# Two levels of Strassen's scheme for a GRU's input products, the inner sums continued in PSUM by ScalarE

## The chip, the cores and the metric

The kernel runs on one core of a Trainium2 chip. The metric is the device time of one execution in microseconds (us). Five engines work at once, each on its own queue of instructions: PE (TensorE, matrix products), DVE (VectorE), ACT (ScalarE), POOL (GpSimd) and SP, which here only starts DMAs. PE reads its operands from the on-chip memory SBUF and writes its products to PSUM; DVE and ACT can read and write both.

## The reference, cut to what matters

Two layers with residual connections. Layer 0 is a gated recurrence that can be computed as a scan over time. Layer 1 is a GRU over 128 steps for 64 batches with width 512, and the change lies there:

```python
xz = jnp.einsum('btd,de->bte', seq, W_z)     # likewise xr with W_r, xh with W
def step(h, xs):
    xzt, xrt, xht = xs
    z = jax.nn.sigmoid(xzt + h @ U_z + vz)   # vz, vr, vh: conditioning and biases
    r = jax.nn.sigmoid(xrt + h @ U_r + vr)
    hh = jnp.tanh(xht + r * h @ U + vh)
    h_new = (1.0 - z) * h + z * hh
    return (h_new, h_new)
```

The products of `seq` (the output of layer 0) with the three weights don't depend on the recurrence and can be made ahead of it. Everything is float32.

## The kernel before, in words

**Layer 0** runs over 16 groups of four batches and four chunks of 128 features (the loop at the file's end). PE multiplies (L186), ACT takes sigmoids, DVE the norm and scans, and the sum x + hidden goes to a DRAM tensor `x2d`, from where it comes back in windows of TW = 16 steps (`load_window`, L469).

**Layer 1** is cut into two streams of 32 batches. Their steps alternate, stream 1 two steps behind. In a step's tiles the partitions are four quarters q of the width by 32 batches, and the free dimension holds j blocks of 32 features. A product with a block of 128 rows of a weight is four matmuls, one for each q, into 32 partitions each (L376); on the chip each float32 matmul is two instructions. `gather` copies four steps of x out of a window into `x4` (ACT) and takes the sums of blocks that Strassen's scheme (in Winograd's form) needs (`s4`, four POOL instructions).

**One step** (`Stream.step`) issues to PE the products of h for r and z into the stream's accumulator `g`, then a fill, then the products of r*h for the candidate. Between them stand ACT's sigmoid (L594), DVE's product r*h (L596) and its transpose (L597), which the candidate's products need. After them come ACT's tanh (L623), `put_share` (L554, the ready share of x for the stream's next step, copied into `g`), DVE's new h and its transpose (L638). `pin` keeps every engine's instructions in the order of the code.

**The fill** makes products of x for later steps. `queue_pair` treats two steps at once as the rows of a 2x2 block matrix, the two halves of the width as its columns, and forms seven products instead of eight; a product is two units of four matmuls with 192 columns (three gates of 64). `fill` issues seven units a step. The products go to halves of PSUM tiles that `product_psum` deals out in turn: a new tile's first half, then its second. One step later DVE (L519) and POOL (L522) add them up to the shares `xz`; `to_read` holds these reads.

The weights' differences for the scheme (`winograd_weights`) are made by DVE in layer 0, one a chunk (L678). The first steps (stream 0 up to 3, stream 1 up to 1) don't use the scheme: `put_v` copies the conditioning into `g`, and `x_products` multiplies x directly, 32 instructions of 384 columns. Where there is nothing to fill with, `idle_products` multiplies zeros.

Ordering between engines is inserted by the framework from the tiles that each instruction reads and writes.

Of the kernel before, what the change touches and what calls it, by code (L numbers as in the profile page):

```python
# [18 lines left out]
def kernel(  # L19
# [23 lines left out]
):  # L43

# [208 lines left out]
    spare = []  # L253

    def chunk_norm(g, c, between=None):
# [17 lines left out]
        if spare:  # L273
            beside.append(spare.pop(0)())
# [51 lines left out]

    def conditioning():

        bias1 = const.tile([P, 3, P], F32, name="bias1")
# [23 lines left out]

        vs = []
        for s in range(2):
            whole = const.tile([P, 3, P], F32, name=f"whole_v{s}")
            pin(nc.vector.tensor_tensor(whole, ps[s], bias1, ALU.add))
            v = const.tile([P, 2, 3, HP], F32, name=f"v{s}")
            halves = whole.rearrange("p g (n e) -> p n g e", n=2)
            pin(nc.scalar.copy(v[:, 0], halves[:, 0]))  # L360
            pin(nc.vector.tensor_tensor(v[:, 1], halves[:, 1], halves[:, 0], ALU.subtract))
            vs.append((whole, v))
# [4 lines left out]
    TW = 16  # L367
# [3 lines left out]
    def matmuls(p, lhsT, w, start=True, stop=True):  # L371

        for k, wk in enumerate(w):
            for q in range(Q):
                pin(
                    nc.tensor.matmul(  # L376
                        p[q * SB : (q + 1) * SB],
                        lhsT=lhsT(k),
                        rhs=part(wk, q),
                        start=(start and k == 0),  # L380
                        stop=(stop and k == len(w) - 1),
                        skip_group_check=True,
                    )
                )

    def winograd_weights():
# [8 lines left out]
        differences = []  # L395
        for k in range(HC):
            differences += [
                (t1[k], b12[k], b11[k]),
                (t2[k], b22[k], t1[k]),
                (t3[k], b22[k], b12[k]),  # L400
                (t4[k], b21[k], t2[k]),
            ]
        return (b11, b21, b22, t1, t2, t3, t4), iter(differences)

    banks = []

    def product_psum():
        if banks:
            return banks.pop()
        n = product_psum.n = product_psum.n + 1  # L410
        p = psum.tile([P, 2, 3, HP], F32, tag=("p1", "p2", "tp")[n % 3], name=f"m{n}")
        banks.append(p[:, 1])
        return p[:, 0]

    product_psum.n = 0
    to_fill = []
    to_read = []

    def fill(n):
        n = min(n, len(to_fill))  # L420
        for _ in range(n):
            unit, reads = to_fill.pop(0)
            unit()
            to_read.extend(reads)
        return n

    def idle_products(n):

        if n:
            p = product_psum()  # L430
            for _ in range(n):
                matmuls(p, lambda _: zeros, w_products[0][:1])

    def read_all():
        while to_read:
            to_read.pop(0)()

    class Stream:
        def __init__(self, s):
# [10 lines left out]

            self.x4 = [const.tile([P, 4, P], F32, name=f"x4_{s}_{n}") for n in range(2)]
            self.s4 = [const.tile([P, 4, 2, HP], F32, name=f"s4_{s}_{n}") for n in range(2)]
            self.windows = {}

        def take_scratch(self, scratch):

            n = 6 * P
            self.xz = [
                scratch[:, m * n : (m + 1) * n].rearrange("p (t g e) -> p t g e", t=2, g=3)
                for m in range(2)  # L460
            ]
            self.sums = scratch[:, 2 * n : 3 * n].rearrange("p (n g e) -> p n g e", n=4, g=3)
# [13 lines left out]
        def gather(self, n):  # L476
            for instruction in self.gather_parts(n):
                instruction()

        def gather_parts(self, n):  # L480

# [3 lines left out]
            x4, s4 = self.x4[n % 2], self.s4[n % 2]  # L485
# [5 lines left out]
            blocks = x4.rearrange("p (m t) (i e) -> p t i m e", t=2, i=2)  # L491
            a11, a12, a21, a22 = (blocks[:, t_, i] for t_ in range(2) for i in range(2))
            s1, s2, s3, s4_ = (s4[:, m] for m in range(4))
            return [
                lambda a=a: pin(nc.gpsimd.tensor_tensor(*a))
# [5 lines left out]
                )  # L501
            ]

        def queue_pair(self, m):

            n, pair = m // 2, m % 2
            x4, s4 = self.x4[n % 2], self.s4[n % 2]
            c1, c2 = (
                [self.xz[m % 2][:, t, :, i * HP : (i + 1) * HP] for i in range(2)] for t in range(2)
            )  # L510
            u, s5, w, u3 = (self.sums[:, i] for i in range(4))
            v1, v21 = self.v[:, 0], self.v[:, 1]
            b11, b21, b22, t1, t2, t3, t4 = w_products

            def block(t, i):
                return x4[:, 2 * pair + t, i * HP : (i + 1) * HP]

            def add(dst, p, other):
                return lambda: pin(nc.vector.tensor_tensor(dst, p, other, ALU.add))  # L519

            def add_beside(dst, a, b_):
                return lambda: pin(nc.gpsimd.tensor_tensor(dst, a, b_, ALU.add))  # L522

            def product(a, w_, reads):
                p = []

                def unit(k):
                    if k == 0:
                        p.append(product_psum())
                    matmuls(  # L530
                        p[0], lambda _: a[:, k * SB : (k + 1) * SB], w_[k : k + 1],
                        start=(k == 0), stop=(k == HC - 1),
                    )

                for k in range(HC):
                    last = k == HC - 1
                    to_fill.append(
                        (
                            (lambda k=k: unit(k)),
                            [lambda: [f() for f in reads(p[0])]] if last else [],  # L540
                        )
                    )

            product(block(0, 0), b11, lambda p: [add(u, p, v1)])
            product(block(0, 1), b21, lambda p: [add(c1[0], p, u)])
            product(s4[:, 1, pair], t2, lambda p: [add(u, p, u)])
            product(s4[:, 0, pair], t1, lambda p: [add(s5, p, v21)])
            product(s4[:, 3, pair], b22, lambda p: [add(w, p, s5), add_beside(c1[1], w, u)])
            product(s4[:, 2, pair], t3, lambda p: [add(u3, p, u), add_beside(c2[1], u3, s5)])
            product(block(1, 1), t4, lambda p: [add(c2[0], p, u3)])  # L550

        def put_share(self, t):

            pin(nc.scalar.copy(self.g, self.xz[t // 2 % 2][:, t % 2]))  # L554
# [16 lines left out]
        def step(self, t, n_fill=7, idle=(0, 0), share=True, filler=None, between=None):  # L571
# [5 lines left out]
            reads = to_read[:]  # L577
            to_read.clear()

            def read(n):  # L580
                for _ in range(min(n, len(reads))):
                    reads.pop(0)()
# [4 lines left out]
            else:  # L587
# [7 lines left out]
                read(1)  # L595
# [4 lines left out]
                pin(nc.gpsimd.tensor_tensor(r, r, h_, ALU.mult))  # L600
            if filler:
                filler()
            fill(n_fill)
# [6 lines left out]
            read(len(reads) - 1)  # L610
# [13 lines left out]
            read(1)  # L624
            if share and t + 1 < S:
# [15 lines left out]
            self.store(t)  # L641

            if t % 4 == 0 and t + 8 <= S and (t > 0 or self.s == 1):
                self.gather(t // 4 + 1)
            if t % TW == 4 and t + TW < S:
                self.load_window(t // TW + 1)
# [17 lines left out]
    for g in range(NG):  # L664
        for c in range(K):
# [10 lines left out]
            if g >= 3:  # L676
                for dst, a, b_ in itertools.islice(sums_of_weights, 1):
                    pin(nc.vector.tensor_tensor(dst, a, b_, ALU.subtract))  # L678
# [5 lines left out]
        if g == 0:  # L684
# [3 lines left out]
            w_products, sums_of_weights = winograd_weights()  # L688
# [5 lines left out]
        if g == NG - 3:  # L694
            spare += streams[0].gather_parts(1)
# [6 lines left out]
    for st in streams:  # L702
        st.take_scratch(flat[:, st.s * 18 * P :])
# [7 lines left out]
    st0.step(0, n_fill=0, share=False)  # L711
# [7 lines left out]
    def step_1(rest):  # L719
        st0.g = g1  # L720
        st0.step(1, n_fill=0, share=False, filler=x_of_step_2, between=rest)
# [5 lines left out]
    st0.queue_pair(2)  # L727
    fill(7)
    st0.step(2, share=False, between=lambda: chunk_retained(g, c))
# [11 lines left out]
    st1.x_products(0)  # L741
    LEAD = 2
    for t in range(LEAD, S + LEAD):
        near_end = t >= S - 3
        n_fill = 4 if near_end else 7
        if t == LEAD + 1:

            st0.step(t, filler=lambda: st1.x_products(1))
        elif LEAD < t < S:
            st0.step(t, n_fill, idle=(0 if to_fill else 4, 0))  # L750
        elif t >= S:
            read_all()

# [43 lines left out]
```

## Time and profile before

| | us |
|---|---|
| median of 3 runs (lowest, highest) | 1974.89 (1974.46, 1975.33) |
| the profiled execution | 1976.27 |
| its span, first to last instruction | 1974.4 |
| first fill of the recurrence, tile m (start) | 722.7 |
| one step of one stream, tanh to tanh | 4.87 |

The page gives the span, each engine's busy time, and the span in 40 slices (a digit is the busy share in tenths; a slice is 49 us). Groups are named by line of the code, engine, operation and tiles; "128*32 128x192" for a matmul is a stationary operand of 128 rows by 32 columns and a moving one of 128 by 192. Timeline rows have the start, the time from the first start to the last end, the engine, the line, the operation, out<-in, the form, the count of merged instructions, and in brackets the engine's idle time before, with what ended it. Tile names are the program's without their numbers: `m` a product, `g` an accumulator, `W` the scratch that `xz` and `sums` live in, `f` the tiles of r, z and r*h.

### The profile page before, as it was taken

Reading aid. Unit: us, or ns where it says so; the run is one execution under the profiler, and the core shown is the slowest. Engines: PE = TensorE matmul, PEld = TensorE weight load, DVE = VectorE, ACT = ScalarE, POOL = GpSimd, SP = SyncE. Lnnn points to the kernel's source line nnn. Section 1 sums busy time; section 2 is a strip of 40 time slices with the busy share of each in tenths; the row PEclk is TensorE's granted clock in tenths of the full one; section 3 lists DMA queues with packets and bytes.
Section 4 is the critical chain, followed back from the end, with each engine's and each line's share of the span. In section 5 each row is a group of like instructions: output and inputs, shape, how many; then the busy total and the mean of one; then the engine's idle time right before and its main releaser. Section 6 shows DMA issues by size and latency. Waiting matters only on the chain.

```text
span 1974.4 us, 73723 instructions
## 1 busy us (share of the span) xinstructions
PE 1958.9 (99%) x32729; PEld 1412.5 (72%) x32729; DVE 1360.5 (69%) x2996; ACT 484.6 (25%) x1108; POOL 752.4 (38%) x1476
## 2 busy tenths in 40 slices
PE   9999999999999999999999999999999999999998
PEld 5444444444444447788888888888888888888887
DVE  6799999999999985555555555555555555555554
ACT  3222212122221222222222222222222222222222
POOL 1222222222233234444444444444444444444443
PEclk9999999999999999999999999999999999999999
DMA  6411111211111211201200220221120121110111
GB/s 202 157 48 48 48 43 54 64 59 49 48 48 43 77 37 24 59 15 19 60 16 14 41 41 14 37 39 20 35 41 14 19 57 19 17 17 14 19 19 19
DMA packets 228407, 84.64 MB, mean 43 GB/s; under 512 B 205484, under 2 KB 205496, under 8 KB 228088
## 3 DMA queue, kind: packets, MB, share of 16 engines
q1 hardware_dynamic: 227488, 79.85, 16.4%
q8 instruction: 257, 4.21, 0.9%
q14 instruction: 62, 0.51, 0.1%
q10 hardware_dynamic: 600, 0.07, 0.0%
HBM read 46.34 MB, written 33.55 MB: 40 GB/s over the span
## 4 chain that ended last, share of the span: by engine, by line
PE 70%; DVE 27%; issue 1%; DMA 1%; ACT 0%; DVEq 0%; SPq 0%; POOL 0%; ACTq 0%; POOLq 0%
PE g L376 34%; PE m L376 29%; DVE h L261 9%; PE p L186 6%; DVE h L312 3%; DVE i L295 3%; DVE h L302 3%; DVE i L294 2%; DVE i L307 2%; DVE f L279 2%; DVE i L282 2%; DVE h L260 2%; DMA cw<-in_L_cond_C_dram 1%; PE tp L144 1%; DMA x<-in_x_dram 0%
## 5 line engine op out<-in xcount | busy, mean ns | idle before, releaser
L186 PE MATMUL p<-xT,W 128*128 128x512 f32 (+1 forms) x1560 | 669.4, 586 | 0.7 <-issue 0.5
L186 PEld LDWEIGHTS p<-xT,W 128*128 128x128 f32 x1560 | 290.0, 190 | 341.7 <-issue 336.4
L376 PE MATMUL g<-w_s,h 128*32 128x256 f32 x8128 | 527.8, 379 | 1.1 <-DVE h L638 1.1
L376 PEld LDWEIGHTS g<-w_s,h 128*32 128x32 f32 x8128 | 336.4, 110 | 98.1 <-ACT g L554 1.8
L376 PE MATMUL m<-w_t,s 128*32 128x192 f32 x6000 | 376.7, 326 | 0.0
L376 PE MATMUL g<-w_s,f 128*32 128x128 f32 x8128 | 311.5, 273 | 2.5 <-DVE f L597 1.5
L630 DVE TENSOR_TENSOR h<-h,f 128x128 f32<-128x128 f32 x254 | 74.3, 292 | 343.7 <-ACT h L623 343.7
L640 POOL TENSOR_TENSOR o<-o,h 128x128 f32<-128x128 f32 x254 | 116.4, 458 | 475.2 <-DVE h L636 466.2
L376 PEld LDWEIGHTS m<-w_t,s 128*32 128x32 f32 x6000 | 263.6, 110 | 21.5 <-issue 0.4
L376 PEld LDWEIGHTS g<-w_s,f 128*32 128x32 f32 x8128 | 270.1, 110 | 10.8 <-issue 4.2
L623 ACT ACTIVATE h<-g 128x128 f32<-128x128 f32 x256 | 70.9, 277 | 697.7 <-PE g L376 697.7
L261 DVE RECIPROCAL h<-h 128x517 f32<-128x517 f32 x64 | 217.0, 3391 | 2.2
L519 DVE TENSOR_TENSOR W<-m,W 128x192 f32<-128x192 f32 x625 | 202.3, 339 | 20.3 <-PE m L376 3.2
L376 PE MATMUL m<-w_x,x 128*32 128x192 f32 x4000 | 206.8, 326 | 0.0
L265 POOL COPY first<-condT 128x4 f32<-128x4 f32 x64 | 12.1, 190 | 508.6 <-DVE h L260 494.0
L596 DVE TENSOR_TENSOR f<-f,h 128x128 f32<-128x128 f32 x254 | 86.2, 339 | 146.9 <-ACT f L594 146.9
L376 PEld LDWEIGHTS m<-w_x,x 128*32 128x32 f32 x4000 | 164.0, 110 | 21.2 <-issue 0.4
L281 ACT ACTIVATE f<-f 128x512 f32<-128x512 f32 x64 | 40.4, 631 | 452.6 <-DVE f L279 452.6
L599 POOL TENSOR_SCALAR f<-f 128x128 f32<-128x128 f32 x254 | 75.5, 297 | 195.6 <-DVE f L596 195.6
L594 ACT ACTIVATE f<-g 128x256 f32<-128x256 f32 x254 | 97.3, 383 | 201.1 <-PE g L376 198.2
L522 POOL TENSOR_TENSOR W<-W 128x192 f32<-128x192 f32 x250 | 143.5, 595 | 1.6 <-DVE W L519 1.5
L376 PE MATMUL m<-w_x,s 128*32 128x192 f32 x2000 | 125.8, 326 | 0.0
(79 smaller groups left out, 2008.2 us busy)
## 6 DMA issues: line engine op xcount, KB each, us to landing
x<-in_x_dram SPq DMA_DIRECT2D x64, 256.0 KB, 3.0
x2d<-x SPq DMA_DIRECT2D x63, 256.0 KB, 2.0
out_dram<-o SPq DMA_DIRECT2D x248, 64.0 KB, 2.0
xw<-x2d SPq DMA_DIRECT2D x60, 256.0 KB, 4.8
w_rows<-in_L_cond_W_f_dram SPq DMA_DIRECT2D x4, 256.0 KB, 5.5
w_rows<-in_L_cond_W_i_dram SPq DMA_DIRECT2D x4, 256.0 KB, 6.4
w_rows<-in_L_cond_W_h_dram SPq DMA_DIRECT2D x4, 256.0 KB, 5.6
w_s<-in_L_cond_U_r_dram SPq DMA_DIRECT2D x1, 1024.0 KB
```

Of the source, the lines that this page charges most:

```text
L186: nc.tensor.matmul(p[:, tokens], lhsT=W0[:, c, n, k, :], rhs=xT[g][:, k, tokens], start=(k == 0), stop=(k == K - 1),)
L261: pin(nc.vector.reciprocal(h, h))
L295: pin(nc.vector.tensor_tensor_scan(i, i, f, 0.0, ALU.add, ALU.mult))
L376: nc.tensor.matmul(p[q * SB : (q + 1) * SB], lhsT=lhsT(k), rhs=part(wk, q), start=(start and k == 0), stop=(stop and k == len(w) - 1), ski ...
L519: return lambda: pin(nc.vector.tensor_tensor(dst, p, other, ALU.add))
L522: return lambda: pin(nc.gpsimd.tensor_tensor(dst, a, b_, ALU.add))
L594: pin(nc.scalar.activation(rz, g[:, RZ], AF.Sigmoid))
L596: pin(nc.vector.tensor_tensor(rh, r, h_, ALU.mult))
L599: pin(nc.gpsimd.tensor_scalar(r, z, -1.0, 1.0, ALU.mult, ALU.add))
L623: pin(nc.scalar.activation(hh, g[:, 2], AF.Tanh))
L630: pin(nc.vector.tensor_tensor(hh, hh, z, ALU.mult))
L640: pin(nc.gpsimd.tensor_tensor(o, o, h, ALU.add))
```

## The change

The unit becomes a group of four steps. Its 4x2 blocks pass through two levels: an outer level of seven products, and within each an inner level of seven, with 96 columns and one block of 128 rows each. The inner level's partial sums stay in PSUM: a product is written or accumulated, ACT copies the sum to the place of the other result that shares it, and PE accumulates on. The outer products of a group are begun two, two, two and one in four consecutive steps, and each is finished in the step after. Five PSUM tiles hold outer products (`banks`); a sixth, cut in five `spots`, takes the products that ACT copies out. The core of the diff:

```diff
-    TW = 16
+    TW = 8
...
+    OPERANDS = (
+        (("x", 0, 0), 0), (("x", 0, 1), 1), (("s", 1), 4), (("s", 0), 3), (("s", 3), 2),
+        (("s", 2), 5), (("x", 1, 1), 6),
+    )
...
+    class Outer:
...
+            self.r = banks[Outer.count % len(banks)]
+            Outer.count += 1
+            st.need_sums(group, self.left[0] == "s")
...
+        def at(self, m, j):
+            return self.r[:, m, :, j, :]
+
+        def spot(self):
+            spots.append(spots.pop(0))
+            return spots[-1]
...
+        def first(self):
+            if not self.inner:
+                return self.plain(0)
+            p = self.spot()
+            product(p, self.a(0, 0), self.w[0][0], start=True)
+            pin(nc.scalar.copy(self.r[:, 0], p.unsqueeze(2).to_broadcast([P, 3, 2, C])))
+
+        def second(self):
+            if self.inner:
+                product(self.at(0, 1), self.s(1), self.t[1])
+                pin(nc.scalar.copy(self.at(1, 0), self.at(0, 1)))
+
+        def beside_second(self):
+            if self.inner:
+                product(self.at(0, 0), self.a(0, 1), self.w[1][0])
+
+        def third(self):
+            if not self.inner:
+                return self.plain(1)
+            product(self.at(1, 0), self.s(2), self.t[2])
+            pin(nc.scalar.copy(self.at(1, 1), self.at(1, 0)))
+
+        def beside_third(self):
+            if self.inner:
+                product(self.at(0, 1), self.s(3), self.w[1][1])
+                spot = self.spot()
+                product(spot, self.s(0), self.t[0], start=True)
+                commons.append(commons.pop(0))
+                self.common = commons[-1]
+                pin(nc.scalar.copy(self.common, spot))
+
+        def fourth(self):
+            if self.inner:
+                product(self.at(1, 0), self.a(1, 1), self.t[3])
+            to_read.append(self.read)
+
+        def read(self):
...
+                pin(nc.vector.tensor_tensor(second, second, common, ALU.add))
...
+            pin(nc.vector.tensor_tensor(dst, r, other, ALU.add))
...
+    def product(out_, a, w_, start=False):
+
+        for q in range(Q):
+            pin(
+                nc.tensor.matmul(
+                    out_[q * SB : (q + 1) * SB],
+                    lhsT=a,
+                    rhs=w_[:, :, q * C : (q + 1) * C],
+                    start=start,
+                    stop=True,
+                    skip_group_check=True,
+                )
+            )
...
+    def take_banks():
+
+        banks.extend(
+            psum.tile([P, 2, 3, 2, C], F32, tag=tag, name=f"bank{n}")
+            for n, tag in enumerate(("p1", "p1", "tp", "p2", "p2"))
+        )
+        rest = psum.tile([P, 5, 3, C], F32, tag="tp", name="spots")
+        spots.extend(rest[:, n] for n in range(5))
...
+    def fill(new):
+
+        old = running[:]
+        running.clear()
+        for o in old:
+            o.third()
+        for o in new:
+            o.first()
+        for o in old:
+            o.beside_third()
+        for o in old:
+            o.fourth()
+        for o in new:
+            o.second()
+        for o in new:
+            o.beside_second()
+        running.extend(new)
...
+    def direct(st, t):
+
+        return t < (8 if st.s == 0 else 4)
...
-            if g >= 3:
-                for dst, a, b_ in itertools.islice(sums_of_weights, 1):
-                    pin(nc.vector.tensor_tensor(dst, a, b_, ALU.subtract))
+            if g >= 3 and c % 2 == 0:
+                subtracts(early_differences, 1)
...
-    st0.queue_pair(2)
-    fill(7)
-    st0.step(2, share=False, between=lambda: chunk_retained(g, c))
+    st0.step(2, between=lambda: chunk_retained(g, c))
...
+    for n in range(1, S // 4):
+        counts = (2, 2, 2, 1)
...
+            at = 2 * (4 * n - 3 + 2 * st.s)
+            ps = group(st, n)
+            for m, count in enumerate(counts if isinstance(counts[0], int) else counts[st.s]):
+                slots.setdefault(at + m, []).extend(itertools.islice(ps, count))
```

Besides: `gather` now queues twelve POOL sums a group (four for each of three sets of blocks), which `take_sums` issues four a step, after POOL's own work on r and z and ahead of the fill. DVE makes 12 more weight differences of 384 elements during layer 0 (outer and inner ones together 20, one every second chunk) and 16 late ones, two after each step, at the start of the recurrence; `group` leaves outers plain (two products of 192 columns, no copies) where their inner differences don't exist yet: all seven of stream 1's first group and four of stream 0's. `read(1)` of the finished outers comes after the new h's transpose, the rest after the next step's fill. `x_products` takes six more steps (stream 0 up to 7, stream 1 up to 3). Windows hold 8 steps instead of 16, and `load_window` asks two windows ahead at the start of one.

## The prediction

> **What bounds the kernel now.** I read the page first (the span, the engines' shares, the span in 40 slices), then the chain that ended last, then the timeline of one step, then the costliest groups with shapes kept apart.
>
> ```profile
> span 1974.4 us, 73723 instructions
> PE 1958.9 (99%) x32729; PEld 1412.5 (72%) x32729; DVE 1360.5 (69%) x2996; ACT 484.6 (25%) x1108; POOL 752.4 (38%) x1476
> PE   9999999999999999999999999999999999999998
> DVE  6799999999999985555555555555555555555554
> PE 70%; DVE 27%; issue 1%; DMA 1%; ACT 0%; DVEq 0%; SPq 0%; POOL 0%; ACTq 0%; POOLq 0%
> ```
>
> TensorE is busy throughout. DVE's row has its nines in slices 2 to 14, layer 0, which the change hardly touches. From about 740 us on the recurrence runs, DVE falls to 5, and the chain is PE alone. One step there ("slot": a step of one stream; the two streams alternate), on PE, ScalarE and VectorE:
>
> ```profile
> 1206.83 1.93 PE L376 MATMUL g<-w_s,h 128*32 128x256 f32 x31
> 1208.39 1.51 PE L376 MATMUL m<-w_x,x 128*32 128x192 f32 x29
> 1208.81 0.38 ACT L594 ACTIVATE f<-g 128x256 f32<-128x256 f32 x1 [0.94 <-PE g L376]
> 1209.55 0.32 DVE L597 STREAM_TRANSPOSE f<-f 128x128 f32<-128x128 f32 x1
> 1209.85 1.02 PE L376 MATMUL m<-w_t,s 128*32 128x192 f32 x20
> 1210.66 0.27 PE L376 MATMUL g<-w_s,f 128*32 128x128 f32 x1
> ```
>
> The r,z products begin at 1206.66 (their first one stands on a row before these), the fill (x's products, tile m) at 1208.39, the candidate's products (g<-w_s,f) at 1210.66. So r,z: 32 instructions in 1.73 us, 54 ns each; fill: 56 in 2.27, 40.5 ns each; candidate: 32 in 0.88 (to 1211.54), 27.5 ns each. Together 4.88, the slot. The three cadences are one price, 0.211 ns a column. ScalarE's sigmoid runs from 0.42 to 0.80 after the fill's start; the transpose that the candidate needs is done at 1209.87, 1.48 after it. The fill thus covers that chain with 0.8 us to spare: what the fill loses is gained, down to 1.5 us, and what it gains is lost.
>
> **The products alone.** Per group (four steps of one stream, so four slots) the fill was 4 x 56 = 224 instructions of 192 columns, 4 x 2.27 = 9.08 us. It becomes 7 x 7 products of 8 instructions of 96 columns, 392. Layer 1's conditioning ran that shape:
>
> ```profile
> 57.77 2.88 PE L344 MATMUL pv<-cw,condT 128*32 128x96 f32 x129 [0.62 <-DMA cw<-in_L_cond_C_dram]
> ```
>
> Each takes 0.246, so the last of 129 began 2.63 after the first: 20.5 ns apart, again 0.211 a column. A product of 8 is 0.163 us, 49 of them 8.0. Alone that would save 1.08 us a group. [...]
>
> **The copies.** Each outer product adds four ScalarE copies out of PSUM: `first` (192 written), `second`, `third` and `common` (96 each). From the rows of ScalarE's COPYs, 12 elements 0.168, 256 0.363, 384 0.483: 96 take 0.24, 192 take 0.32. 28 a group are 7.3 us, 1.8 a slot beside the 1.14 of sigmoid, tanh and share: ScalarE has room. What counts is who waits. Each copy stands between two products, and all five `spots` are slices of one PSUM tile (`rest`), each outer's sums another. Is a tile handed over whole, or by the bytes touched? One place of before answers:
>
> ```profile
> 728.33 0.83 PE L376 MATMUL m<-w_t,x 128*32 128x192 f32 x16
> 737.32 1.48 PE L376 MATMUL m<-w_x,x 128*32 128x192 f32 x32
> 738.22 0.36 DVE L519 TENSOR_TENSOR W<-m,W 128x192 f32<-128x192 f32 x1 [2.24 <-PE m L376]
> ```
>
> This read takes a pair's seventh product, finished at 729.16; DVE stood idle 2.24 us before it, released by PE. Halves of a tile are dealt out in turn (`product_psum`), so an odd product's partner is the next pair's first: 16 of the 32 matmuls at 737.32, cadence (1.48-0.33)/31 = 37 ns, the sixteenth ending at 738.20. The read began 0.02 later. It waited for a write to the other half. So I take it that a PSUM tile changes hands whole, in program order; the other end, by bytes, is a rival. [...]
>
> The price of one turn:
>
> ```profile
> 709.37 0.85 PE L376 MATMUL g<-w_s,zeros 128*32 128x384 f32 x8
> 710.29 0.48 ACT L558 COPY g<-whole_v 128x384 f32<-128x384 f32 x1 [0.53 <-PE g L376]
> 710.83 0.53 PE L376 MATMUL g<-w_x,x 128*32 128x384 f32 x4 [0.60 <-ACT g L558]
> ```
>
> Eight matmuls of 384 columns take 0.85, of which 8 x 384 x 0.211 = 0.65 is streaming and 0.20 drain; of 96 columns 0.163 + 0.20 = 0.36. Then 0.06 to the copy and 0.06 back to PE. So a copy starts 0.42 after its product, and PE goes on 0.06 after the copy's end: a turn is 0.42 + 0.24 + 0.06 = 0.72 with a short copy, 0.80 with a long one.
>
> **A slot with two old outers (a, b) and two new ones (c, d)**, in the order of `fill`, zero at its first matmul. ScalarE is in order: sigmoid to 0.80, then with 0.03 between them third a 0.83-1.07, third b 1.10-1.34, first c 1.37-1.69. PE has done third a, b and first c by 0.49. First d needs the spots' tile: 1.75; its copy 2.17-2.49. Beside_third a: spot 2.55, common copy 2.97-3.21. Beside_third b: spot 3.27, copy 3.69-3.93. Meanwhile fourth a, b to 3.76, second c 3.76, second d 3.92-4.08; copies 4.18-4.42 and 4.45-4.69; beside_second c 4.48, d 4.75, end **4.91** (14 products; cadence alone 2.28).
> Two new, one old, the same way: third copied by 1.07, first c by 1.42, first d 1.48 with copy to 2.22, spot 2.28, fourth and second c, d to 2.93, copies to 3.26 and 3.53, end **3.75**. One new, two old: first c copied by 1.69, spots 1.75 and 2.47, fourths and second c to 3.12, copy to 3.62, end **3.84**.
> Counts go 2, 2, 2, 1, so a group is 2 x 4.91 + 3.75 + 3.84 = 17.4 us against 9.08: **+8.3**, 2.1 us a slot. The candidate's chain (1.5 us) hides inside; nothing hides the waits, as all PE work behind them is in order.
>
> Groups: 30 of stream 0, 31 of stream 1, 427 outers, of which 11 stay plain (the first groups): 416/7 = 59.4 groups x 8.33 = +495.
>
> **The rest.** Six more steps take x directly (32 instructions of 384 columns, 81 ns: 2.6 instead of 2.27): +2. Weight differences: twelve early ones of 384 elements and sixteen late ones on DVE (a 384-element DVE add took 0.54); the early ones, 6.5 us, lie where DVE is nearly full: 0 to +6, I take +1. Removed PSUM reads (14 of 0.33 a group) give way to 7 x (0.34 + 0.55): 1.6 us a slot against 1.2, with DVE's 2.7 a slot (27.5 busy in 49) then 3.1 of 7. POOL's sums go from 4 to 12 a group (0.47 each), +0.94 a slot, on 2.2 (22.2 in 49) 3.2 of 7; needed a slot later: nothing, and at the old period still under 4.9. A bank's read (0.9 us, one to two slots after `fourth`) precedes its reuse after five outers. SP: windows of half the length, twice the transfers, issued some 16 slots ahead against 4.8 us to landing: nothing; without that cover each of some 28 windows would cost about 5. Spread: layer 0's step 2 loses its two fills (up to -4).
>
> Sum: the profiled execution took 1976.3 (span 1974.4, 1.9 around it); 1976.3 + 495 + 3 = 2474; the median of the runs, 1974.89, lies 1.4 below it. I say **2475**.
>
> **Bounds of the turn.** A group's chain holds 14 turns (4, 4, 3, 3). PE after a DVE instruction took 0.15 (1957.11 to 1957.26) rather than 0.06, and an SBUF copy of 192 0.351 rather than 0.32: +0.12 a turn at most, 1.7 a group, +100. Downward, half the drain hidden: -0.10, -85; and if ScalarE's third copies cost PE less than supposed, another -40. Own range 2340 to 2620.
>
> **Rivals.**
> 1. *By bytes* (waits only where data are shared). Second c at 1.75, second d at 2.10, end 2.59; the others 2.32 and 2.07 (sigmoid ahead of the copies holds them): 9.57 a group, +0.49 x 59.4 = +29: **2008**. Against it: the read at 738.22.
> 2. *The spots apart, each outer's own tile whole.* First d no longer waits; ends 3.34, 2.80, 2.99: 12.5, +3.4 x 59.4: **2178**. Same objection.
> 3. *Faster: the copies come in time and PE alone decides.* 8.0 for 9.08, -1.08 x 59.4 + 3: **1914**. It decides only if first's copy ends before PE reaches second, 1.6 us into the fill; with the sigmoid till 0.80 and two third copies before it that holds for no `second` by the rows (1.69 and 2.04).
> That the change doesn't do what it says: if most outers stayed plain, the time would be about 1975; the loop makes only 11 so.
>
> **Chances.** Whole tiles 0.84, rivals 0.06, 0.04, 0.05, unchanged 0.01. The range is the first case's own, 2340 to 2620, which leaves out the rivals (0.16) and little more. Faster by over 0.2% (what a measurement here can tell from none) 0.05, within 0.2% 0.01, slower 0.94.
>
> **What would show it.** Right: PE's busy share in the recurrence falls to some two thirds, its idle time in front of `bank` and `spots` matmuls released by ACT copies, some 2 us a slot; slots of 7.5, 7.5, 6.4, 6.4 us; 96-column matmuls 20.5 ns apart inside a product; the r,z and candidate products unchanged. Wrong: PE still at 99%, or ACT copies and products of one tile overlapping in time; then rival 1 or 3. The prediction falls if PE can write one spot while ScalarE reads another.

## The result, and the profile after

The changed kernel takes 2362.89 us (median of 4 runs, 2362.21 to 2363.21) against 1974.95: 1.1964 times as long, 95% interval 1.1943 to 1.1985. That is 388 us slower; 500 were forecast. Its profiled execution has a span of 2360.4 us, 386 above before's.

From the page of the kernel after: span, busy times, the rows of PE and ACT over the slices, the chain.

```profile
span 2360.4 us, 95855 instructions
PE 2089.1 (89%) x42665; PEld 1321.3 (56%) x42665; DVE 1466.0 (62%) x2992; ACT 831.9 (35%) x2770; POOL 930.8 (39%) x1824
PE   9999999999998888888888888888888888888888
ACT  3122121221212344444444444444444444444442
PE 62%; DVE 18%; ACT 14%; issue 5%; DMA 1%; ACTq 0%; DVEq 0%; SPq 0%; POOL 0%; POOLq 0%
```

The nines of PE end where the recurrence begins (between 900 and 1900 us PE was busy for 1.00 of the time before, 0.83 after), and ACT, which held 0% of the chain, holds 14%. Who waited for whom on PE (total us, times, longest):

```profile
PE spots L536 <- ACT bank L473: 138.0, 350, 0.6
PE bank L536 <- ACT bank L478: 67.1, 240, 0.7
PE spots L536 <- ACT i L497: 17.0, 88, 0.2
```

L473 is `first`'s copy, L478 `second`'s, L497 the common one. (A matmul's modelled end covers 0.2 us of each wait, so these sums are too small: eight matmuls 20.5 ns apart, 0.163 us, show as 0.37 in the rows below.) From tanh to tanh the four steps of a group last 6.94, 6.99, 6.04 and 5.90 us, 25.87 together, against 19.51. Over the 53 groups of the middle that is 337 us; the first 24 steps add 34, the last 19 add 15: the 386.

One full fill, PE's and ACT's rows of the timeline:

```profile
1501.69 0.51 PE L536 MATMUL bank<-w_inner,ss 128*32 128x96 f32 x16
1501.94 0.38 ACT L722 ACTIVATE f<-g 128x256 f32<-128x256 f32 x1 [0.93 <-PE g L374]
1502.02 0.35 PE L536 MATMUL spots<-w_t,s 128*32 128x96 f32 x8
1502.22 0.39 ACT L488 COPY bank<-bank 128x96 f32<-128x96 f32 x2
1502.52 0.31 ACT L473 COPY bank<-spots 128x192 f32<-128x192 f32 x1
1502.88 0.37 PE L536 MATMUL spots<-w_t,s 128*32 128x96 f32 x8 [0.51 <-ACT bank L473]
1503.68 0.37 PE L536 MATMUL spots<-w_inner,ss 128*32 128x96 f32 x8 [0.26 <-ACT bank L473]
1504.41 0.37 PE L536 MATMUL spots<-w_inner,ss 128*32 128x96 f32 x8 [0.19 <-ACT border L497]
1505.68 0.54 PE L536 MATMUL bank<-w_t,s 128*32 128x96 f32 x16 [0.23 <-ACT bank L478]
1506.03 1.05 PE L374 MATMUL g<-w_s,f 128*32 128x128 f32 x32
```

The fill lasts from 1501.69 to 1506.03, 4.34 us for 14 products of 0.163. A slot with two old and two new outers has four products into the spots; here they begin at 1502.02, 1502.88, 1503.68 and 1504.41, the last three each 0.05 us after a copy out of another spot of the same tile has ended (1502.83, 1503.62, 1504.36). Those copies share no byte with the products that wait for them.

### The profile page after: what moved, and what is told of

It is laid out like the page before. It is cut to its first block, busy times and chain, and to the rows that moved or that the text cites. A ratio compares the mean times of both kernels' runs of the same rounds, so it can differ in the third digit from the quotient of the medians.

```text
span 2360.4 us, 95855 instructions
## 1 busy us (share of the span) xinstructions
PE 2089.1 (89%) x42665; PEld 1321.3 (56%) x42665; DVE 1466.0 (62%) x2992; ACT 831.9 (35%) x2770; POOL 930.8 (39%) x1824
## 4 chain that ended last, share of the span: by engine, by line
PE 62%; DVE 18%; ACT 14%; issue 5%; DMA 1%; ACTq 0%; DVEq 0%; SPq 0%; POOL 0%; POOLq 0%
PE g L374 30%; PE bank L536 11%; PE spots L536 10%; PE p L187 10%; DVE h L260 6%; ACT bank L473 5%; ACT f L722 3%; ACT bank L478 2%; DVE h L309 2%; DVE i L292 2%; DVE h L299 2%; ACT bank L488 2%; DVE i L291 1%; DVE i L304 1%; DVE f L276 1%
## 5 line engine op out<-in xcount | busy, mean ns | idle before, releaser
L374 PEld LDWEIGHTS g<-w_s,h 128*32 128x32 f32 x8128 | 259.1, 110 | 134.8 <-ACT g L687 1.8
L374 PEld LDWEIGHTS g<-w_s,f 128*32 128x32 f32 x8128 | 220.3, 110 | 4.7 <-issue 2.6
L536 PE MATMUL spots<-w_inner,ss 128*32 128x96 f32 x2856 | 133.0, 258 | 64.0 <-ACT bank L473 30.0
L536 PE MATMUL bank<-w_inner,ss 128*32 128x96 f32 x5712 | 184.6, 246 | 0.5 <-ACT bank L473 0.5
L526 DVE TENSOR_TENSOR W<-bank,W 128x384 f32<-128x384 f32 x305 | 169.6, 556 | 10.3
L536 PEld LDWEIGHTS bank<-w_inner,ss 128*32 128x32 f32 x5712 | 143.5, 110 | 32.7 <-issue 1.0
L473 ACT COPY bank<-spots 128x192 f32<-128x192 f32 x416 | 127.3, 306 | 91.2 <-PE spots L536 91.2
L536 PEld LDWEIGHTS spots<-w_inner,ss 128*32 128x32 f32 x2856 | 56.3, 108 | 138.9 <-ACT bank L473 66.5
L727 POOL TENSOR_TENSOR f<-f,h 128x128 f32<-128x128 f32 x254 | 116.3, 458 | 21.2
L687 ACT COPY g<-W 128x384 f32<-128x384 f32 x244 | 117.9, 483 | 11.0
```

What stands on the lines that cost most here:

```text
L374: nc.tensor.matmul(p[q * SB : (q + 1) * SB], lhsT=lhsT(k), rhs=part(wk, q), start=(start and k == 0), stop=(stop and k == len(w) - 1), ski ...
L473: pin(nc.scalar.copy(self.r[:, 0], p.unsqueeze(2).to_broadcast([P, 3, 2, C])))
L526: pin(nc.vector.tensor_tensor(dst, r, other, ALU.add))
L536: nc.tensor.matmul(out_[q * SB : (q + 1) * SB], lhsT=a, rhs=w_[:, :, q * C : (q + 1) * C], start=start, stop=True, skip_group_check=True,)
L687: pin(nc.scalar.copy(self.g, self.xz[:, t // 2 % 2, t % 2]))
```

## The experiments

Three theories were to be told apart: PE stands through each handover of a whole PSUM tile; the time is the work itself (more copies, more and smaller matmuls); or the rest of the change (regrouping, POOL's sums, windows) costs it.

**e1: the order within a fill.**

```diff
-        for o in old:
-            o.third()
-        for o in new:
-            o.first()
-        for o in old:
-            o.beside_third()
...
+            (old, "third"), (new, "first"), (old, "common_product"),
+            (old, "third_copy"), (new, "first_copy"), (old, "common_copy"),
+            (old, "beside_third"), (old, "fourth"), (new, "second"), (new, "beside_second"),
```

`third`, `first` and `beside_third` lose their copies, and `beside_third` its product into a spot; these are now steps of their own (`third_copy`, `first_copy`, `common_product`, `common_copy`).

> Same products, copies, tiles and sums as the change; only the order within a fill differs: all products into the spots (first of the new outers, common of the old) come one after another before ScalarE's copies out of them. Theory (a PSUM tile changes hands whole, and PE stands through each turn): by the recurrence of the prediction with the measured start of ScalarE's queue, the fills become 2.70, 2.70, 2.35 and 2.37 us, 10.1 a group against 15.5 measured; 5.4 x 59.4 less than 2363, about 2045. Rival A (the time is the work itself: 28 more ScalarE copies a group, 392 small matmuls with their own weight loads): nothing is taken away, so 2363 within 1%. Rival B (PE waits only for data): no product into a spot waits now, so the order changes little, above 2300.

Measured: 2091.1 us, 1.059 of before (1.0574 to 1.0606). The same instructions in another order take 272 us less. Of PE's waits on copies out of the spots one of 0.5 us is left; what remains on ACT is the last handover of each fill, `second`'s:

```profile
PE bank L549 <- ACT bank L482: 64.1, 239, 0.5
```

The work itself (rival A) can't be the cause of those 272, and rival B is out. The median steps are 5.40, 5.38, 5.11 and 5.07: fills some 0.1 above the recurrence, 24 us of the 46 by which the expectation was missed. Another 14 are longer steps at changing places (mean group 21.24, the four medians together 20.97), of which more below.

**e2: the last handover too.** Against e1:

```diff
-            (old, "third"), (new, "first"), (old, "common_product"),
+            (old, "beside_second"), (old, "third"), (new, "first"), (old, "common_product"),
...
-            (old, "beside_third"), (old, "fourth"), (new, "second"), (new, "beside_second"),
+            (old, "beside_third"), (old, "fourth"), (new, "second"),
```

> As e1_spots_together, and besides the product that follows second's copy in the same tile (beside_second) moves to the start of the next step's fill, so that this copy has a whole step. Theory: the last turn of each fill goes too; fills 2.30, 2.30, 1.96 and 1.81 us, 8.4 a group against 9.08 before the change: 0.7 x 59.4 faster than before, about 1935, and faster than both kernels. Rival A (work itself): 2363. Rival C (small matmuls cost more than 20.5 ns each in this setting, or ScalarE's 1.9 us a step comes onto the path of the sigmoid): at or above 1975.

Measured: 2008.46 us, 1.017 (1.0155 to 1.0185). In the fills PE waits for ACT in a few places only, 0.3 us in all between 900 and 1900. The medians of a group's four steps sum to 18.97 us, near the expected 10.44 + 8.37 = 18.81. But the mean group is 19.84: one step in five is 0.4 to 2.1 us longer, at changing places. And the first 24 steps last 17 us longer than before's. So the miss of 73 us is not the handovers: 0.87 in each of 59.4 groups and the start make most of it.

**e3: no copies at all.**

```diff
-            pin(nc.scalar.copy(self.r[:, 0], p.unsqueeze(2).to_broadcast([P, 3, 2, C])))
...
-                product(self.at(0, 1), self.s(1), self.t[1])
-                pin(nc.scalar.copy(self.at(1, 0), self.at(0, 1)))
+                product(self.at(0, 1), self.s(1), self.t[1], start=True)
...
-            pin(nc.scalar.copy(self.at(1, 1), self.at(1, 0)))
...
-                pin(nc.scalar.copy(self.common, spot))
```

> The change without ScalarE's four copies per outer product: all 49 products a group, DVE's and POOL's sums and their order stay; the results of layer 1's products of x are not the reference's. Theory: PE never waits in a fill, which lasts 8.0 us a group by 20.4 ns a matmul; 1.08 x 59.4 below before plus a few, about 1915; the difference to 2363 (450) is all waiting. [...]

Measured: 1996.71 us, 1.0111 (1.0096 to 1.0126), 82 above the theory's place. The medians of the four steps sum to 18.70, 0.8 below before's; 8.0 us of products would make it 18.4. The mean group is 19.73. The long steps have stalls that no semaphore explains ("issue"):

```profile
1311.79 0.64 PE L374 MATMUL g<-w_s,f 128*32 128x128 f32 x16 [0.67 <-issue]
1316.15 1.08 PE L374 MATMUL g<-w_s,f 128*32 128x128 f32 x32 [0.34 <-issue]
```

They come in the candidate's products too, which are as before. The DMA queue q8 of kind instruction moved 333 packets of 16 KB in the kernel after, 257 before: one for about every 256 PE instructions (weight loads and matmuls, 85330 after and 65458 before). Of 87 pauses of over 0.3 us between weight loads (900 to 1850 us), nine in ten end 1.21 to 1.60 us after such a packet; moments at random lie 0.2 to 3.8 after one.

**e4: no inner level.**

```diff
-            if (st.s, n) == (1, 1):
...
-                inner = True
+            inner = False
```

> The change with every outer product made plain (two products of 192 columns, no inner level, no copies); groups of four steps, windows of 8, twelve POOL sums a group, 36 weight differences and the first direct steps stay. Theory: PE's work is before's, 9.08 us a group, so 1980, within 10: the rest of the change costs next to nothing. Rival D (the regrouping, POOL's sums or the smaller windows cost a part of the 388 us): 2050 or more.

Measured: 2001.44 us, 1.0136 (1.0119 to 1.0153): 27 above before, more than the theory's 10 and less than rival D's 75. The first 24 steps take 14 of it (direct products of x and fills meet there, and before's two fills beside layer 0's last chunk are gone). Then every fourth step is 0.24 longer than its PE work, 12 over the 53 groups of the middle. A place of that kind, POOL's, DVE's and PE's rows:

```profile
1310.57 1.00 POOL L528 TENSOR_TENSOR W<-W 128x384 f32<-128x384 f32 x1 [0.33 <-DVE W L526]
1310.70 1.02 DVE L723 TENSOR_TENSOR f<-f,h 128x128 f32<-128x128 f32 x1 [0.21 <-ACT f L722]
1311.75 0.31 DVE L724 STREAM_TRANSPOSE f<-f 128x128 f32<-128x128 f32 x1
1312.21 1.03 PE L374 MATMUL g<-w_s,f 128*32 128x128 f32 x29
```

DVE's r*h takes 1.02 us rather than 0.29 beside POOL's add, and the candidate's products begin 0.15 after its transpose. The fill's 48 matmuls, at 40.5 ns each from 1310.01, would have let them begin at 1311.95, 0.25 earlier.

**e5: short matmuls in the kernel before.** Each unit of a fill is cut in two:

```diff
+                    for j in range(2):
+                        for q in range(Q):
...
+                                    p[0][q * SB : (q + 1) * SB, :, j * C : (j + 1) * C],
+                                    lhsT=a[:, k * SB : (k + 1) * SB],
+                                    rhs=part(w_[k], q)[:, :, j],
```

> The kernel before with each 192-column matmul of the fill cut in two of 96 columns: the same columns, sums and waits, but 112 instructions with their weight loads in place of 56 a step, and no ScalarE copies. In the run without copies PE stood still at places that no semaphore explains, each time going on 1.2 to 1.6 us after a 16 KB fetch on the DMA queue of kind instruction had ended (one fetch per 256 PE instructions). Theory F (PE's instructions arrive too late for bursts of such short matmuls): matmuls still 20.4 ns apart inside a burst, but stalls of that kind appear; 128 pairs then take some 3.6 us on average as in the run without copies, whose stalls were 34 us in 1000; 1990 to 2050. Rival (those stalls came from the copies' program, or DVE and POOL): within 0.5% of 1975. [...]

Measured: 2059.87 us, 1.0428 (1.0414 to 1.0443), 10 above theory F's range and far from the rival's (no effect). Undisturbed steps last 4.91 (before 4.88), so the 112 short matmuls take 2.27 + 0.03 us there, 20.5 ns each; but the mean group is 20.92 against 19.51. A line of PE's timeline, its longest stall there (the packet ahead of it had ended at 1336.28):

```profile
1337.91 0.28 PE L533 MATMUL m<-w_x,x 128*32 128x96 f32 x3 [2.10 <-issue]
```

The instruction queue's line on its page (packets, MB, share):

```profile
q8 instruction: 366, 6.00, 1.2%
```

Of 93 pauses nine in ten end 1.25 to 1.58 us after a packet. The trace allows a sharper test: from each pause to the next PE issues a multiple of 256 instructions (weight loads, matmuls and its sequencer's own), within 2, in all 92 cases, and in 81 of 83 in e3 (pauses that end 1.15 to 1.75 us after a packet). (A step has 352 weight loads and matmuls, so its own rhythm doesn't make this.) The pauses keep to the packets' size. That PE stops where one packet's instructions end, for want of the next, is my reading; the trace doesn't show which instructions a packet holds. The stalls belong to short matmuls, not to the copies or the regrouping.

**e6: four inner outers of seven.** In `group`, on e2: `inner = i % 2 == 0`.

> As e2_beside_next_step, but only outers 0, 2, 4 and 6 of a group go through the inner level; 1, 3 and 5 are plain (32 instructions of 192 columns). Each inner outer saves 1.30 - 1.14 = 0.15 us of PE, 0.6 a group, 37 us; the start costs the 12 that the all-plain run showed, and its 0.24 us in every fourth step may stay (14). Instructions on PE fall to 88 pairs in a full fill from 112, so stalls by late instructions should be rare. Theory: 1950 to 1965, faster than before. Rival: if the stalls stay as in e2_beside_next_step (23 us in 1000), 1980 to 1995.

Measured: 2034.43 us, 1.0303 (1.0289 to 1.0317): both expectations missed. The long steps are gone (mean and median group both 20.30), but 20.30 is 1.4 above PE's work: plain products stood between the products into the spots, so the copies out of that tile began late and PE waited for them again (between 900 and 1900 us ACT's `first` copy waited 212 us in all for products into the spots; PE waited 76 times on `first`'s copies, and 23 times on POOL's sums).

**e7: plain products as cover.** The order of a fill:

```diff
+            (old, "beside_second"), (old, "third"), (new, "first"), (old, "common_product"),
+            (old, "third_copy"), (new, "first_copy"), (old, "common_copy"),
+            (old, "plain_third"), (new, "plain_first"),
+            (old, "beside_third"), (old, "fourth"), (new, "second"),
```

> As e6_half_of_outers_inner, but in a fill the inner outers' products before the copies (beside_second, third, first, common) all come first, then the plain outers' 192-column products, then what needs the copies (beside_third, fourth, second). e6's steps lasted 20.3 us a group where PE's work is 18.9 (10.44 + 8.46); the 1.4 is PE behind copies out of the spots, whose start was late because plain products stood between the two products into the spots' tile. Theory: with the plain products as cover no turn is waited for; 18.9 to 19.2 a group against 19.5 before, plus 12 at the start: 1945 to 1970, faster than before by 0.2 to 1.5%. Rival (POOL's 384-element add of a share holds DVE's r*h, 1.02 us in place of 0.29 as in one step in four of the all-plain run): 0.24 to 0.4 a group more, up to 1990.

Measured: 1955.73 us, 0.99 (0.9886 to 0.9915): faster than before. The median group is 18.92, as forecast (18.9 to 19.2), the mean 18.94. The order of the fill is all that differs from e6.

**e8: POOL's adds to the shares one step later.** On e7: `read` puts the adds in a list, and `step` issues them after POOL's work on r and z.

> As e7_plain_as_cover, but POOL's two adds of 384 elements a group (to the shares) are issued after the next step's POOL work on r and z instead of right after DVE's read, so that they no longer run beside DVE's r*h. If that meeting costs e7 anything, this one is 5 to 20 us faster than e7 and DVE's r*h takes 0.29 throughout; if not, equal within 0.2%.

Measured: 1953.47 us, 0.9889 (0.9873 to 0.9906). DVE's r*h now takes 0.290 on average (0.336 in e7), but the time falls by 2.3 us only, 0.12%. In the profiled executions that is not in the recurrence's middle, which takes 1005.2 us against e7's 1004.1: with these fills the meeting was not on the path. This is the fastest version, 21 us below before:

```profile
span 1952.3 us, 86324 instructions
PE 1934.1 (99%) x38417; PEld 1499.3 (77%) x38417; DVE 1407.0 (72%) x2815; ACT 689.2 (35%) x2062; POOL 935.8 (48%) x1824
```

PE is at 99% again, and its instructions (38417 matmuls) are fewer than the 42665 of the full scheme.

## Why the prediction was right in kind and too high by 112 us

- **A PSUM tile changes hands whole: right.** Products into one spot waited for copies out of another in every fill, and e1 took 272 us back by order alone. The single read at 738.22 in before's trace had pointed to it. Every one of these waits is for a semaphore that the framework put in; whether the chip itself would bear a finer order wasn't tried.
- **The price of a turn: right.** 0.80 with `first`'s copy and 0.73 with the common one, from 1502.88 to 1503.68 and 1504.41; forecast 0.80 and 0.72. PE's busy share came to 0.83, not two thirds: the modelled ends cover some 0.2 us in each of 14 turns, 2.8 of a group's 25.87 us, and the group is shorter than forecast.
- **The step that failed: when ScalarE's queue gets going.** "ScalarE is in order: sigmoid to 0.80, then with 0.03 between them third a 0.83-1.07, third b 1.10-1.34, first c 1.37-1.69", and so first d at 1.75. Measured, the sigmoid ran from 0.25 to 0.63 after the fill's first matmul, the three copies were done at 1.14, and first d began at 1.19. Of the 0.56, 0.17 lies in the point from which the forecast counts, and the rest in the spacing. The sigmoid is no earlier against the products that it reads: it begins 0.43 after the start of the last r,z matmul before, 0.45 after (medians), but the fill's first matmul, the forecast's zero, begins 0.005 behind that r,z matmul before and 0.20 behind it after. And ACT's instructions don't stand 0.03 apart here, as `put_share` behind tanh does (0.03 to 0.09): each begins 0.08 to 0.10 before the one ahead has ended. Before's trace had that in layer 0, where I didn't look:

```profile
675.71 0.63 ACT L281 ACTIVATE f<-f 128x512 f32<-128x512 f32 x1 [8.50 <-DVE f L279]
676.25 0.67 ACT L232 ACTIVATE f<-p,biasT 128x512 f32<-128x512 f32 x1
```

The first ends at 676.34, the second begins at 676.25. All four fills begin with this chain: steps less 2.61 of other products leave 4.33, 4.38, 3.43 and 3.29 for the forecast 4.91, 4.91, 3.84 and 3.75. That is 2.0 a group, 118 us over 59.4 groups; the start below, 14 instead of next to nothing, works the other way, and together they make nearly all of the 112.
- **That 2363 lies inside the range is luck in part.** The room below 2475 was given for half the drain hidden and for cheaper third copies. The turns came out whole; the 112 come from a term for which the range had no room.
- **"The rest" at +3: too low.** It was 27 (e4): the start 14, where I had +2 for the direct steps and up to -4 for the lost fills, and 12 for the meeting of POOL and DVE, where I had written that POOL's longer queue costs nothing. In the changed kernel itself that meeting doesn't occur: its r*h takes 0.291 on average.
- **Rival 3's 1914, PE alone: wrong in its price.** e3, without a wait for a copy, takes 1997. The cadence of 20.5 ns is right inside a burst, but the price had no term for the stalls, which lengthen e3's mean group by 1.0 us. In the fill above the matmuls start in fours, 7 ns apart, with 82 ns from four to four: 20.5 is a mean.
- **Two slips on which nothing hangs:** DVE's nines stand in slices 3 to 14, not 2 to 14, and the sum of 2474 less 1.4 is 2473, not 2475.

## What to carry to other kernels

Before partial sums are continued in PSUM by another engine, list per PSUM tile who touches it in program order; every change of engine there cost a turn here (0.73 to 0.80 us), whichever bytes were meant. Put all writes of one engine to a tile together, then the other's reads, and in between work on other tiles: that order was worth 272 us, and plain products as cover (e7) made the scheme pay at all. Fewer multiplications in 1.75 times the instructions may lose in stalls what they gain on columns: e2's and e3's undisturbed steps sum to less than before's (18.97 and 18.70 against 19.50), the kernels were slower.

## What the runs showed of the hardware

- **PE's stalls keep step with the instruction queue.** With pairs of weight load and matmul 20.4 ns apart, stalls without a semaphore appear, a multiple of 256 PE instructions apart (92 of 92 in e5, 81 of 83 in e3), and end 1.2 to 1.6 us after a 16 KB packet of the instruction queue. The mean group is longer than its four median steps by 1.0 us in e3, 1.1 in e5, 0.9 in e2, 0.01 at 40.5 ns (before) and 0.05 where long and short matmuls mix (e8). A packet took about 1.1 us, and no two began less than 3.3 us apart in e3 and e5 (900 to 1850 us), while 128 pairs at 20.4 ns last 2.6. That PE outruns its instructions is my reading of these numbers. Why the next packet would come late, how many of them lie ahead of PE, and whether other DMA traffic takes part, no run here shows.
- **DVE's r*h took longer beside POOL's add of 384 elements:** 1.02 us for 0.29 in e4, and on average 0.488 in e4, 0.336 in e7 and, with the add issued later, 0.290 in e8. The add itself took 1.00 us in that place of e4 and 1.01 on average in e8. This cost 12 us in e4, and between e7 and e8 nothing that shows in the recurrence.
- **ACT's instructions can overlap by about 0.1 us** in the profile: 0.09 in layer 0, 0.08 to 0.10 in the fill above. Where `put_share` follows tanh, whose tile it overwrites, it begins 0.03 to 0.09 after tanh's end; what makes the difference wasn't tried.
